# Four-layer graph network on 64 graphs: the multiplication order of layers 1 and 2, the places of right operands and kept blocks, and bias and mask on GpSimd

## The chip, the cores and the metric

The kernel runs on one core of one Trainium2 chip. The time is device microseconds of one execution. The kernel before took 2791.32 us (median of 3 runs, 2790.5 to 2792.68).

TensorE (PE in the profile, PEld its weight loads) multiplies matrices, VectorE (DVE), ScalarE (ACT) and GpSimd (POOL) do the rest, and SyncE (SP) issues all the transfers. Each engine runs its own instructions in order and waits for the others by semaphores.

## The reference

The input `x` is 64 graphs of 256 nodes with 512 features, `adj` a 256x256 matrix for each graph. Each of four layers adds its result to `x`. All is in float32.

```python
# h = relu(layernorm(x)) ahead of each layer; x = x + layer(h, adj)
# layer 0
Wh = h @ W;  e = leaky_relu(Wh @ a1 + (Wh @ a2).T)
attention = softmax(where(adj > 0.5, e, NEG_INF), axis=1)
out = elu(attention @ Wh)
# layer 1
Ah = adj + eye;  dh = rsqrt(sum(Ah, -1))
out = relu((dh[:, None] * Ah * dh[None, :]) @ h @ kernel + bias)
# layer 2
mask = any(h != 0, -1)
out = relu(adj @ h @ kernel) * mask
# layer 3
out = relu(concat([h, (adj @ h) / max(deg, EPS)], -1) @ W.T)
```

## The kernel before

**Block products.** Every matrix product is made by the scheme of Strassen and Winograd on 2x2 blocks: 7 block products in place of 8, with sums on both sides. A left operand has seven places (`A11, A12, S1, A22, S2, S4, S3`, line 33), a right one too (`B11, T4N, B22, T1, T3, T2, B21`, line 36). The function `project` (line 533) issues the seven products into three PSUM banks `z`, `y` and `v`; `snap` copies a bank out while the sum in it goes on, `add` adds a bank to a block that was copied before, and `last` takes the final block straight from the bank. Where no places are given, the blocks copied out are kept in a tile `c` of their own (line 539).

**Two orders of multiplying.** A layer needs adjacency times `h` times weights.

- *Aggregated* (`aggregate`, line 472): first 8 matmuls of 128x128x256 give the transpose of adjacency times `h` in two banks (line 482); `left_sums` (line 458) copies it into a tile `xw` and makes its sums; then 7 products of two chunks, 14 matmuls, with the weights.
- *Turned* (`turn`, line 619, and `neighbours`, line 651): `h` is transposed in 32x32 blocks on VectorE, written to DRAM (`hd`, one transfer) and read back in turned order (`hw`, four transfers); 14 matmuls with the weights give the right operand `y`; `differences` (line 256) makes its sums; then a `Gathered` operand multiplies by the adjacency in 7 matmuls. The sums of the adjacency's blocks come from `block_sums` (line 671) on GpSimd, in tiles `aw`.

Before, layers 0, 2 and 3 are turned and layer 1 is aggregated, in every graph. Layer 3 has also the product of `h` with the other half of its weights in the same banks, 35 matmuls in all. In the first FIRST = 2 graphs (line 25) `h` of layer 0 is transposed by TensorE (line 722) and not through DRAM.

**Around the products.** `norm` (line 394) is the layernorm with relu. In layer 1, VectorE copies the blocks out with row scale and bias in one instruction (line 804), adds the others with `dh` (line 811), and adds relu of them to `xs` (line 816). In layer 0, `off` (line 750) is the mask of the softmax; `deg` and `mask` (lines 708 and 839) are small instructions of VectorE.

**The order of the instructions** comes from a planner (class `Plan`, line 47). Each instruction is recorded with an engine, an estimated duration and what it reads and writes. Durations are multiplied by STRETCH per engine (line 28). Due times come from the graph's number times APART, with the last LAST graphs pulled ahead by LATE (line 365). The planner then places all the instructions by list scheduling, with a fixed number of buffers for each kind of tile (line 890), and they are issued in the order of their planned starts. Engines, PSUM banks and buffers of many graphs so interleave: at any time several graphs are in work.

Of the kernel before, what the change touches and what calls it, by code (L numbers as in the profile page):

```python
# [24 lines left out]
FIRST = 2  # L25
LAST, LATE = 2, 0.5

STRETCH = {"DVE": 1.1, "ACT": 1.03, "POOL": 1.25, "PE": 1.0, "DMA": 1.0}
# [7 lines left out]
B11, T4N, B22, T1, T3, T2, B21 = range(7)  # L36
# [117 lines left out]
def kernel(  # L154
# [39 lines left out]
    class Tiles:  # L194
# [61 lines left out]
    def differences(op, engs, tile, key, late=()):  # L256

        steps = ((slice(T1, T3 + 1), slice(B12, B22 + 1), slice(B11, B12 + 1), (B11, B12, B22), (T1, T3)),
                 (T2, B22, T1, (B22, T1), (T2,)),
                 (T4N, B21, T2, (B21, T2), (T4N,)))  # L260
        for (eng, us), (to, i, j, reads, writes) in zip(engs, steps):
            on = nc.vector if eng == "DVE" else nc.gpsimd
            op(eng, us, lambda g, on=on, to=to, i=i, j=j: on.tensor_tensor(  # L263
                tile(g)[:, to], tile(g)[:, i], tile(g)[:, j], ALU.subtract),
               [key(n) for n in reads], [key(n) for n in writes], **dict(late))
# [97 lines left out]
    def graph(b):  # L363
# [83 lines left out]
        def more_sums(xw):  # L447
            put = lambda *n: [f"{xw}.{i}" for i in n]
            op("DVE", 0.43, lambda g: nc.vector.tensor_tensor(  # L449
                g[xw][:, S2], g[xw][:, S1], g[xw][:, A11], ALU.subtract),  # L450
               put(S1, A11), put(S2), urgent=True)
            flat = lambda t: t.rearrange("p b k n -> p b (k n)")
            op("POOL", 1.45, lambda g: nc.gpsimd.tensor_tensor(  # L453
                flat(g[xw][:, S4 : S3 + 1]), flat(g[xw][:, A12 : A22 + 1 : A22 - A12]),
                flat(g[xw][:, S2 : S2 + 1]).to_broadcast([P, 2, FH * P]), ALU.subtract),
               put(A12, A22, S2), put(S3, S4), urgent=True)

        def left_sums(lo, hi, xw):

            declare(xw, [P, 7, FH, P], tag="xw")  # L460
            put = lambda *n: [f"{xw}.{i}" for i in n]
            op("ACT", 0.59, lambda g: nc.scalar.copy(
                g[xw][:, A12 : A22 + 1 : A22 - A12].rearrange("p h k n -> p k h n"),
                g[hi].rearrange("p k (h n) -> p k h n", h=NC)), [hi], put(A12, A22), urgent=True)
            op("ACT", 0.38, lambda g: nc.scalar.copy(g[xw][:, A11], g[lo][:, :, :P]),
               [lo], put(A11), urgent=True)
            op("DVE", 0.43, lambda g: nc.vector.tensor_tensor(
                g[xw][:, S1], g[lo][:, :, P:], g[xw][:, A22], ALU.add),
               [lo] + put(A22), put(S1), urgent=True)
            more_sums(xw)  # L470
# [23 lines left out]
        PLACE = {(0, 0): 0, (0, 1): 1, (1, 1): 2}  # L494

        class Weighted:


            def __init__(self, x, w):
                self.x, self.w, self.chunks = x, w, FH  # L500

            def left(self, g, at, k):
                return g[self.x][:, at, k]
# [7 lines left out]
        class Gathered:  # L511
# [21 lines left out]
        def project(operands, l, keep, keep_us, total, last, also=[], places=None, width=OH):  # L533
# [3 lines left out]
            if places is None:  # L537
                kept = f"c{l}"
                declare(kept, [P, 3, OH], tag="c")
                places = {ij: (lambda g, at=at: g[kept][:, at], f"{kept}.{ij[0]}{ij[1]}")  # L540
                          for ij, at in PLACE.items()}
# [52 lines left out]
        def both(t):  # L594

            return t[:, 0:2].rearrange("p a o -> p (a o)")

        def pieces(l):  # L600
            kept = f"c{l}"
            if l < 3:
                declare(f"total{l + 1}", [P, 3], tag="total")
            return (
                (1, "10", lambda g: g[f"pz{l}"], [f"pz{l}"], lambda g: quarter(g["xs"], 1, 0), ["xs.10"], 256, 1),
                (1, "11", lambda g: g[kept][:, 2], [f"{kept}.11"], lambda g: quarter(g["xs"], 1, 1), ["xs.11"], 256, 2),
                (0, "0", lambda g: both(g[kept]), [f"{kept}.00", f"{kept}.01"], lambda g: g["xs"][:, 0, :], ["xs.00", "xs.01"], 512, 0),
            )
# [10 lines left out]
        def turn(l):  # L619


            h, hw = f"h{l}", f"hw{l}"
            for c in (1, 0):
                op("DVE", 0.71, lambda g, c=c: nc.vector.transpose(g[h][:, c, :], g[h][:, c, :]),  # L624
                   [f"{h}.{c}"], [f"{h}.{c}"])
            hd, G = f"hd{l}", P // Q
            declare(hd, [N * F], tag="hd")
            op("DMA", 512, lambda g: nc.sync.dma_start(
                g[hd].rearrange("(p x) -> p x", p=P), g[h].rearrange("p c f -> p (c f)")),
               [f"{h}.0", f"{h}.1"], [hd], holds=0.45, lands=5.0)  # L630
            declare(hw, [P, 7, FH, P], tag="xw")
            for q in range(G):
                op("DMA", 128, lambda g, q=q: nc.sync.dma_start(
                    g[hw][q * Q : (q + 1) * Q, : 2 * NC].rearrange("j s k (a r) -> j (s k) a r", r=Q),
                    g[hd].rearrange("(a j x q r) -> q j x a r", a=G, j=Q, q=G, r=Q)[q]),
                   [hd], [f"{hw}.q{q}"], holds=0.85, lands=4.5)
            op("DVE", 0.48, lambda g: nc.vector.tensor_tensor(
                g[hw][:, S1], g[hw][:, S1], g[hw][:, A22], ALU.add),
               [f"{hw}.q{q}" for q in range(G)], [f"{hw}.{i}" for i in (A11, A12, A22, S1)], urgent=True)
            more_sums(hw)  # L640
# [10 lines left out]
        def neighbours(l, w, by=None, x=None, width=OH):  # L651


            y = f"y{l}"
            declare(y, [P, 7, width], tag="y")
# [10 lines left out]
            project([Weighted(x or f"hw{l}", w)], f"y{l}", keep, 0.38, total, last, also, places=places,  # L666
# [4 lines left out]
        def block_sums(l, a):  # L671
# [5 lines left out]
                g[aw][:, 0], block(g, 0, 1), block(g, 1, 1), ALU.add), [a] + ([f"h{l}.0"] if l else []), [f"{aw}.{S1}"])  # L677
# [30 lines left out]
        op("DVE", 0.18, lambda g: nc.vector.tensor_scalar_max(g["deg"], g["deg"], EPS_DEG),  # L708
# [41 lines left out]
        op("DVE", 0.48, lambda g: nc.vector.tensor_scalar(  # L750
# [19 lines left out]
        def elu0(i, key, y, y_keys, to, to_keys, n, at, tag):  # L770
            us = 0.42 if n == 256 else 0.61
            ex = f"ex{tag}"
            declare(ex, [P, n], tag=f"ex{n}")
# [10 lines left out]
        first, second, third = pieces(0)  # L784
        block_sums(0, "e")
        project([Gathered("e", "aw0", "y0")], 0, plain_keep, 0.38, plain_total, lambda _: elu0(*first, "a"))
# [8 lines left out]
            flat(g["ahT"])[:, P : 3 * P], flat(g["aT"])[:, P : 3 * P]), ["aT", "total1.0"], ["ahT.off"])  # L795
        for c in range(NC):
# [3 lines left out]
               ["aT", "=ident", "total1.0"], [f"ahT.{c}"])  # L800
        aggregate("h1", "ahT", 1, ["ahT.off", "ahT.0", "ahT.1"])
# [6 lines left out]
        def scaled_keep(i, j):  # L808
            return "DVE", lambda g, to, block: scaled(g, i, to, block, j)

        scaled_total = (0.49, lambda g, i, to, block: nc.vector.scalar_tensor_tensor(
            to, block, g["dh"][:, i : i + 1], to, ALU.mult, ALU.add))
# [7 lines left out]
        first, second, third = pieces(1)  # L820
# [6 lines left out]
        project([Weighted("xw1", 1)], 1, scaled_keep, 0.49, scaled_total, last1, ["dh", "=bias"])  # L827
# [11 lines left out]
        op("DVE", 0.17, lambda g: nc.vector.tensor_scalar(g["mask"], g["mask"], 0.0, None, ALU.is_gt),  # L839
# [3 lines left out]
        turn(2)  # L843
        neighbours(2, 2)
        block_sums(2, "aT")
# [9 lines left out]
        _, second, third = pieces(2)  # L855
        keep, total = row_scaled("mask")
        project([Gathered("aT", "aw2", "y2")], 2, keep, 0.38, total, last2, ["mask.0", "mask.1"])
# [7 lines left out]
        block_sums(3, "aT")  # L865
# [9 lines left out]
        project([Weighted("hw3", 3), Gathered("aT", "aw3", "y3")], 3, keep, 0.38, total, last3, ["rdeg"])  # L875
        _, second, third = pieces(3)
# [11 lines left out]
    for b in range(B):  # L888
        graph(b)
    buffers = dict(  # L890
        xs=8, a_nat=1, ab=1, aT=6, h=3, mva=5, xw=3, c=3, off=1, junk=1, ex256=3, ex512=1,
        a_rows=1, a_cols=1, turned=1, row=16, hd=8, y=3, pl=1, ps=8,
# [37 lines left out]
```

## Time and profile before

| | before |
|---|---|
| median of 3 runs | 2791.32 us |
| the profiled execution | 2790.29 us |
| its span | 2788.5 us |
| granted TensorE clock, mean | 0.998 |
| DMA queue q1 | 1018668 packets, 313.56 MB, 48.1% of 16 engines' time |
| HBM | 180.23 MB read, 133.23 MB written |

Times in the profile are microseconds from the start of the span, unless marked ns. A group of instructions is given by line, engine, operation, tiles written and read (buffer numbers left out), shape and count; then its busy time, the mean of one in ns, and the idle time of its engine just before. A float32 matmul leaves two records in the trace, so counts of MATMUL are twice the matmuls that the kernel issues.

### The profile page before, as it was taken

The numbers are of one execution on the slowest core, as the hardware profiler recorded it, in microseconds if no ns is written. First come the engines' busy times: TensorE is split into PE (matmuls) and PEld (weight loads), VectorE is DVE, ScalarE is ACT, GpSimd is POOL, SyncE is SP. The second block draws the span as 40 slices with busy tenths as digits, with TensorE's granted clock in tenths as the row PEclk, the third lists the DMA queues.
The fourth block names the chain that finished last, engine by engine and source line by source line (L and its number), as shares of the span: only waits on it lengthen the run. The fifth ranks groups of instructions, "written<-read, shape, count | busy, mean of one in ns | idle before, by whom it ended". The sixth has DMA issues, their size and how long they took to land.

```text
span 2788.5 us, 43020 instructions
## 1 busy us (share of the span) xinstructions
PE 2766.1 (99%) x12775; PEld 2423.6 (87%) x12775; DVE 2217.1 (80%) x5305; ACT 1782.1 (64%) x4318; POOL 1464.1 (53%) x2582
## 2 busy tenths in 40 slices
PE   7999999999999999999999999999999999999999
PEld 6888888888888888888888888888888888888887
DVE  6887788778887878878788787887878878778765
ACT  5776666665666666666666666665666666666653
POOL 6764545455454555555455454554645546455542
PEclk9999999999999999999999999999999999999999
DMA  8344454445454444544455444554544545444333
GB/s 223 81 119 118 102 114 118 114 113 124 99 129 115 105 114 107 136 115 106 105 120 119 114 108 112 122 114 108 128 100 120 126 102 131 99 114 98 78 91 76
DMA packets 1018901, 316.31 MB, mean 113 GB/s; under 512 B 933668, under 2 KB 960940, under 8 KB 1018668
## 3 DMA queue, kind: packets, MB, share of 16 engines
q1 hardware_dynamic: 1018668, 313.56, 48.1%
q8 instruction: 103, 1.69, 0.3%
q14 instruction: 130, 1.06, 0.1%
HBM read 180.23 MB, written 133.23 MB: 112 GB/s over the span
## 4 chain that ended last, share of the span: by engine, by line
PE 98%; DVE 1%; DMA 0%; SPq 0%; ACT 0%; issue 0%; POOL 0%; DVEq 0%; POOLq 0%; ACTq 0%
PE pz L551 28%; PE pzy L551 24%; PE pv L551 14%; PE pvy L551 12%; PE pt L482 8%; PE py L551 7%; PE pyy L551 6%; PE pwa_w L318 0%; DMA a_rows_w<-in_L_gnn_a_dram 0%; DMA w3n_w<-in_L_gnn_W_dram 0%; DVE e L752 0%; DVE y L263 0%; DVE h L624 0%; SPq L691 0%; DVE y L592 0%
## 5 line engine op out<-in xcount | busy, mean ns | idle before, releaser
L551 PE MATMUL pzy<-wb,hw 128*128 128x257 f32 (+1 forms) x3040 | 772.0, 380 | 2.7 <-DMA hw<-hd 2.2
L551 PEld LDWEIGHTS pzy<-wb,hw 128*128 128x128 f32 x3040 | 577.3, 190 | 83.1 <-issue 2.6
L443 ACT ACTIVATE h<-xs,nb,rstd 128x512 f32<-128x512 f32 x512 | 398.9, 807 | 34.3 <-POOL nb L440 28.7
L551 PE MATMUL pvy<-wb,hw 128*128 128x256 f32 (+1 forms) x1520 | 382.6, 380 | 0.0
L590 ACT COPY y<-pzy 128x256 f32<-128x256 f32 (+1 forms) x512 | 190.7, 372 | 281.7 <-PE pzy L551 232.7
L551 PEld LDWEIGHTS pvy<-wb,hw 128*128 128x128 f32 x1520 | 289.2, 190 | 40.5 <-DVE y L647 0.4
L453 POOL TENSOR_TENSOR hw<-hw 128x512 f32<-128x512 f32 x190 | 255.4, 1344 | 129.7 <-DVE hw L449 76.2
L422 ACT ACTIVATE h<-xs,mv 128x512 f32<-128x512 f32 x384 | 274.8, 716 | 21.6 <-POOL mv L416 14.1
L624 DVE STREAM_TRANSPOSE h<-h 128x512 f32<-128x512 f32 x380 | 257.3, 693 | 36.0 <-ACT h L443 36.0
L551 PE MATMUL pz<-wb,xw 128*128 128x256 f32 x1024 | 263.0, 379 | 0.8 <-DVE c L804 0.5
L551 PE MATMUL pz<-wb,hw 128*128 128x256 f32 x1024 | 262.8, 379 | 0.6 <-ACT c L645 0.6
L263 POOL TENSOR_TENSOR y<-y 128x256 f32<-128x256 f32 x192 | 156.9, 824 | 171.8 <-DVE y L263 116.3
L482 PE MATMUL pt<-ahT,h 128*128 128x256 f32 x1024 | 237.8, 381 | 2.0 <-POOL y L263 2.0
L263 DVE TENSOR_TENSOR y<-y 128x256 f32<-128x256 f32 (+1 forms) x384 | 231.3, 628 | 7.0
L551 PE MATMUL pz<-y,aw 128*128 128x256 f32 x768 | 228.4, 379 | 0.0
L551 PE MATMUL pv<-y,aw 128*128 128x256 f32 x768 | 228.4, 379 | 0.0
L816 DVE SCALAR_TENSOR_TENSOR xs<-c,xs 128x256 f32<-128x256 f32 (+1 forms) x384 | 221.3, 578 | 3.8
L482 PEld LDWEIGHTS pt<-ahT,h 128*128 128x128 f32 x1024 | 195.6, 191 | 29.2 <-POOL y L263 2.2
L551 PEld LDWEIGHTS pz<-wb,xw 128*128 128x128 f32 x1024 | 194.0, 190 | 28.5 <-POOL rstd L426 0.9
L551 PEld LDWEIGHTS pz<-wb,hw 128*128 128x128 f32 x1024 | 194.2, 190 | 27.7 <-ACT c L645 1.0
L645 ACT ACTIVATE y<-pzy,rdeg 128x256 f32<-128x256 f32 x256 | 120.8, 472 | 143.5 <-PE pzy L551 127.1
L430 POOL TENSOR_TENSOR rstd<-rstd,minus_half 128x2 f32<-128x2 f32 x256 | 199.3, 779 | 19.5
(135 smaller groups left out, 5629.8 us busy)
## 6 DMA issues: line engine op xcount, KB each, us to landing
hd<-h SPq DMA_DIRECT2D x190, 512.0 KB, 2.8
hw<-hd SPq DMA_DIRECT2D x760, 128.0 KB, 3.3
xs<-in_x_dram SPq DMA_DIRECT2D x64, 512.0 KB, 5.3
out_dram<-xs SPq DMA_DIRECT2D x64, 512.0 KB, 3.9
ab<-in_adj_dram SPq DMA_DIRECT2D x256, 64.0 KB, 2.5
a_nat<-in_adj_dram SPq DMA_DIRECT2D x64, 256.0 KB, 3.4
pl<-dpl SPq DMA_DIRECT2D x61, 128.0 KB, 3.2
wb<-in_L_gnn_kernel_dram SPq DMA_DIRECT2D x8, 256.0 KB
```

What stands on the lines that cost most here:

```text
L263: op(eng, us, lambda g, on=on, to=to, i=i, j=j: on.tensor_tensor(tile(g)[:, to], tile(g)[:, i], tile(g)[:, j], ALU.subtract), [key(n) for ...
L422: op("ACT", 1.0, lambda g, c=c: nc.scalar.activation(g[h][:, c, :], g["xs"][:, c, :], AF.Square, bias=g[mv][:, 0, c : c + 1], accum_out=g[ ...
L430: op("POOL", 0.72, lambda g: nc.gpsimd.tensor_tensor(g[rs], g[rs], minus_half, ALU.pow), [rs, "=half"], [rs])
L443: op("ACT", 0.81, lambda g, c=c: nc.scalar.activation(g[h][:, c, :], g["xs"][:, c, :], AF.Relu, bias=g[nb][:, c : c + 1], scale=g[rs][:, c ...
L453: op("POOL", 1.45, lambda g: nc.gpsimd.tensor_tensor(flat(g[xw][:, S4 : S3 + 1]), flat(g[xw][:, A12 : A22 + 1 : A22 - A12]), flat(g[xw][:, ...
L482: nc.tensor.matmul(g[pt][:, kk, :], lhsT=g[h][:, c, k * P : (k + 1) * P], rhs=g[moving][:, c, :], start=(c == 0), stop=(c == NC - 1),)
L551: nc.tensor.matmul(g[t], lhsT=o.left(g, left, k), rhs=o.right(g, right, k), start=start and n == 0, stop=n == len(parts) - 1, skip_group_c ...
L590: return "ACT", lambda g, to, block: nc.scalar.copy(to, block)
L624: op("DVE", 0.71, lambda g, c=c: nc.vector.transpose(g[h][:, c, :], g[h][:, c, :]), [f"{h}.{c}"], [f"{h}.{c}"])
L645: lambda i, j: ("ACT", lambda g, to, block: nc.scalar.activation(to, block, AF.Copy, scale=g[by][:, i : i + 1])),
L816: lambda g, kw: nc.vector.scalar_tensor_tensor(to(g), y(g), 0.0, to(g), ALU.max, ALU.add, **kw), y_keys, to_keys,
```

## The change

Five things change.

1. Layer 1 is turned in graphs 8 to 61 and aggregated in the others; layer 2, turned in all before, is now turned in graphs 8 to 61 and aggregated in the first eight and the last two.
2. Right operands of layers 1 and 2 are written into the places of the left operand `hw` that was used up (`y = f"hw{l}"`), and the kept blocks into places of an operand already used (`kept`); the tile `c` is gone. The places of the right operand are ordered anew, with T1 and T3, B11 and T4N, T4N and B22 two places apart. Block sums of the adjacency are made once for layers 2 and 3 in the turned graphs (`aw2`).
3. From graph 8 on, ScalarE copies layer 1's blocks with the row scale, and GpSimd adds the bias (`biased`).
4. On GpSimd in place of VectorE: `off` from graph 8 on, the maximum of `deg`, the comparison of `mask`.
5. The planner's figures: FIRST 3, LAST 3, LATE 0.3, STRETCH, and the buffers (`aT` 7, `xw` 4, no `c`, `ex256` 2).

```diff
-FIRST = 2
-LAST, LATE = 2, 0.5
-STRETCH = {"DVE": 1.1, "ACT": 1.03, "POOL": 1.25, "PE": 1.0, "DMA": 1.0}
+FIRST = 3
+LAST, LATE = 3, 0.3
+STRETCH = {"DVE": 1.06, "ACT": 1.06, "POOL": 1.15, "PE": 1.0, "DMA": 1.0}
...
-B11, T4N, B22, T1, T3, T2, B21 = range(7)
+B11, T1, T4N, T3, B22, T2, B21 = range(7)
...
-        steps = ((slice(T1, T3 + 1), slice(B12, B22 + 1), slice(B11, B12 + 1), (B11, B12, B22), (T1, T3)),
+        steps = ((slice(T1, T3 + 1, 2), slice(B12, B22 + 1, 2), slice(B11, B12 + 1, 2), (B11, B12, B22), (T1, T3)),
...
         class Weighted:
+                self.kept = x, (A11, S1, S2)
...
         class Gathered:
+                self.kept = y, (B11, T1, T3)
...
             if places is None:
-                kept = f"c{l}"
-                declare(kept, [P, 3, OH], tag="c")
-                places = {ij: (lambda g, at=at: g[kept][:, at], f"{kept}.{ij[0]}{ij[1]}")
-                          for ij, at in PLACE.items()}
+                kept, at = operands[-1].kept
+                places = {ij: (lambda g, n=n: g[kept][:, n, :OH], f"{kept}.{n}")
+                          for ij, n in zip(((0, 0), (0, 1), (1, 1)), at)}
...
                 op(eng, keep_us, lambda g: fn(g, at(g), g[f"p{bank}{l}"]),
                    [f"p{bank}{l}"] + also, [key], urgent=True)
+                if kept_then:
+                    kept_then(i, j, at, key)
...
-            y = f"y{l}"
-            declare(y, [P, 7, width], tag="y")
+            if l in (1, 2):
+                y = f"hw{l}"
+            else:
+                y = f"y{l}"
+                declare(y, [P, 7, width], tag="y")
...
-        op("DVE", 0.18, lambda g: nc.vector.tensor_scalar_max(g["deg"], g["deg"], EPS_DEG),
+        op("POOL", 0.3, lambda g: nc.gpsimd.tensor_scalar_max(g["deg"], g["deg"], EPS_DEG),
...
-        op("DVE", 0.48, lambda g: nc.vector.tensor_scalar(
+        op(*(("POOL", 1.0) if b >= 8 else ("DVE", 0.52)), lambda g: (nc.gpsimd if b >= 8 else nc.vector).tensor_scalar(
             g["off"], g["aT"], 0.5, 0.5, ALU.is_gt, ALU.subtract), ["aT"], ["off"])
...
-        aggregate("h1", "ahT", 1, ["ahT.off", "ahT.0", "ahT.1"])
+        if 8 <= b < B - 2:
+            turn(1)
+            neighbours(1, 1)
+            block_sums(1, "ahT")
+            operands = Gathered("ahT", "aw1", "hw1")
+        else:
+            aggregate("h1", "ahT", 1)
+            operands = Weighted("xw1", 1)
...
+        def biased(i, j, at, key):
+            op("POOL", 0.8, lambda g: nc.gpsimd.tensor_tensor(
+                at(g), at(g), bias[:, j * OH : (j + 1) * OH], ALU.add), [key, "=bias"], [key], urgent=True)
...
-        project([Weighted("xw1", 1)], 1, scaled_keep, 0.49, scaled_total, last1, ["dh", "=bias"])
+        if b >= 8:
+            keep, total = row_scaled("dh")
+            project([operands], 1, keep, 0.48, total, last1, ["dh"], kept_then=biased)
+        else:
+            keep = lambda i, j: ("DVE", lambda g, to, block: scaled(g, i, to, block, j))
+            total = row_scaled("dh")[1]
+            project([operands], 1, keep, 0.49, total, last1, ["dh", "=bias"])
...
-        op("DVE", 0.17, lambda g: nc.vector.tensor_scalar(g["mask"], g["mask"], 0.0, None, ALU.is_gt),
+        op("POOL", 0.3, lambda g: nc.gpsimd.tensor_scalar(g["mask"], g["mask"], 0.0, None, ALU.is_gt),
...
-        turn(2)
-        neighbours(2, 2)
-        block_sums(2, "aT")
+        if 8 <= b < B - 2:
+            turn(2)
+            neighbours(2, 2)
+            block_sums(2, "aT")
+            gathered = Gathered("aT", "aw2", "hw2")
+        else:
+            aggregate("h2", "aT", 2)
+            gathered = Weighted("xw2", 2)
...
-        block_sums(3, "aT")
+        if not 8 <= b < B - 2:
+            block_sums(2, "aT", 3)
...
-        xs=8, a_nat=1, ab=1, aT=6, h=3, mva=5, xw=3, c=3, off=1, junk=1, ex256=3, ex512=1,
-        a_rows=1, a_cols=1, turned=1, row=16, hd=8, y=3, pl=1, ps=8,
+        xs=8, a_nat=1, ab=1, aT=7, h=3, mva=5, xw=4, off=1, junk=1, ex256=2, ex512=1, a_rows=1,
+        a_cols=1, turned=1, row=16, hd=8, y=3, pl=1, ps=8,
```

More of the change, by code (lines that the diff above doesn't have):

```diff
@@ L451, in more_sums @@
                put(S1, A11), put(S2), urgent=True)
-            flat = lambda t: t.rearrange("p b k n -> p b (k n)")
             op("POOL", 1.45, lambda g: nc.gpsimd.tensor_tensor(
-                flat(g[xw][:, S4 : S3 + 1]), flat(g[xw][:, A12 : A22 + 1 : A22 - A12]),
-                flat(g[xw][:, S2 : S2 + 1]).to_broadcast([P, 2, FH * P]), ALU.subtract),
+                g[xw][:, S4 : S3 + 1], g[xw][:, A12 : A22 + 1 : A22 - A12],
+                g[xw][:, S2 : S2 + 1].to_broadcast([P, 2, FH * P]), ALU.subtract),
                put(A12, A22, S2), put(S3, S4), urgent=True)
         def left_sums(lo, hi, xw):
-            declare(xw, [P, 7, FH, P], tag="xw")
+            chunks = lambda t: t.rearrange("p (k n) -> p k n", k=FH)
+            declare(xw, [P, 7, OH], tag="xw")
             put = lambda *n: [f"{xw}.{i}" for i in n]
             op("ACT", 0.59, lambda g: nc.scalar.copy(
-                g[xw][:, A12 : A22 + 1 : A22 - A12].rearrange("p h k n -> p k h n"),
+                g[xw][:, A12 : A22 + 1 : A22 - A12].rearrange("p h (k n) -> p k h n", k=FH),
                 g[hi].rearrange("p k (h n) -> p k h n", h=NC)), [hi], put(A12, A22), urgent=True)
-            op("ACT", 0.38, lambda g: nc.scalar.copy(g[xw][:, A11], g[lo][:, :, :P]),
+            op("ACT", 0.38, lambda g: nc.scalar.copy(chunks(g[xw][:, A11]), g[lo][:, :, :P]),
                [lo], put(A11), urgent=True)
             op("DVE", 0.43, lambda g: nc.vector.tensor_tensor(
-                g[xw][:, S1], g[lo][:, :, P:], g[xw][:, A22], ALU.add),
+                chunks(g[xw][:, S1]), g[lo][:, :, P:], chunks(g[xw][:, A22]), ALU.add),
                [lo] + put(A22), put(S1), urgent=True)
@@ L492, in aggregate @@
             left_sums(f"pt{l}_0", f"pt{l}_1", f"xw{l}")
-        PLACE = {(0, 0): 0, (0, 1): 1, (1, 1): 2}
         class Weighted:
@@ L500, in __init__ @@
                 self.x, self.w, self.chunks = x, w, FH
+                self.kept = x, (A11, S1, S2)
             def left(self, g, at, k):
-                return g[self.x][:, at, k]
+                return g[self.x][:, at, k * P : (k + 1) * P]
             def right(self, g, at, k):
@@ L531, in keys, with project @@
                 return [of, f"{self.y}.{right}"]
-        def project(operands, l, keep, keep_us, total, last, also=[], places=None, width=OH):
+        def project(operands, l, keep, keep_us, total, last, also=[], places=None, width=OH,
+                    kept_then=None):
             if places is None:
-                kept = f"c{l}"
-                declare(kept, [P, 3, OH], tag="c")
-                places = {ij: (lambda g, at=at: g[kept][:, at], f"{kept}.{ij[0]}{ij[1]}")
-                          for ij, at in PLACE.items()}
+                kept, at = operands[-1].kept
+                places = {ij: (lambda g, n=n: g[kept][:, n, :OH], f"{kept}.{n}")
+                          for ij, n in zip(((0, 0), (0, 1), (1, 1)), at)}
             for t in "zyv":
@@ L592, in graph, with pieces @@
         plain_total = (0.43, lambda g, i, to, block: nc.vector.tensor_tensor(to, block, to, ALU.add))
[L594 to L601, printed above, removed]
+        def pieces(l, operands):
+            kept, (p00, p01, p11) = operands.kept
             if l < 3:
@@ L605, in pieces @@
                 (1, "10", lambda g: g[f"pz{l}"], [f"pz{l}"], lambda g: quarter(g["xs"], 1, 0), ["xs.10"], 256, 1),
-                (1, "11", lambda g: g[kept][:, 2], [f"{kept}.11"], lambda g: quarter(g["xs"], 1, 1), ["xs.11"], 256, 2),
-                (0, "0", lambda g: both(g[kept]), [f"{kept}.00", f"{kept}.01"], lambda g: g["xs"][:, 0, :], ["xs.00", "xs.01"], 512, 0),
+                (1, "11", lambda g: g[kept][:, p11, :OH], [f"{kept}.{p11}"], lambda g: quarter(g["xs"], 1, 1), ["xs.11"], 256, 2),
+                (0, "0", lambda g: g[kept][:, p00 : p01 + 1 : p01 - p00, :OH], [f"{kept}.{p00}", f"{kept}.{p01}"],
+                 lambda g: g["xs"][:, 0, :].rearrange("p (j o) -> p j o", o=OH), ["xs.00", "xs.01"], 512, 0),
             )
@@ L630, in turn @@
                [f"{h}.0", f"{h}.1"], [hd], holds=0.45, lands=5.0)
-            declare(hw, [P, 7, FH, P], tag="xw")
+            declare(hw, [P, 7, OH], tag="xw")
             for q in range(G):
                 op("DMA", 128, lambda g, q=q: nc.sync.dma_start(
-                    g[hw][q * Q : (q + 1) * Q, : 2 * NC].rearrange("j s k (a r) -> j (s k) a r", r=Q),
+                    g[hw][q * Q : (q + 1) * Q, : 2 * NC].rearrange("j s (a r) -> j s a r", r=Q),
                     g[hd].rearrange("(a j x q r) -> q j x a r", a=G, j=Q, q=G, r=Q)[q]),
@@ L664, in last @@
                    urgent=True)
-            project([Weighted(x or f"hw{l}", w)], f"y{l}", keep, 0.38, total, last, also, places=places,
+            project([Weighted(x or f"hw{l}", w)], f"h{l}", keep, 0.38, total, last, also, places=places,
                     width=width)
@@ L669, in neighbours, with block_sums @@
                         lambda i: f"{y}.{i}", dict(urgent=True))
-        def block_sums(l, a):
+        def block_sums(l, a, when=None):
             aw = f"aw{l}"
@@ L676, in block_sums @@
             op("POOL", 0.5, lambda g: nc.gpsimd.tensor_tensor(
-                g[aw][:, 0], block(g, 0, 1), block(g, 1, 1), ALU.add), [a] + ([f"h{l}.0"] if l else []), [f"{aw}.{S1}"])
+                g[aw][:, 0], block(g, 0, 1), block(g, 1, 1), ALU.add), [a] + ([f"h{when or l}.0"] if l else []), [f"{aw}.{S1}"])
             op("POOL", 0.5, lambda g: nc.gpsimd.tensor_tensor(
@@ L772, in elu0 @@
             ex = f"ex{tag}"
-            declare(ex, [P, n], tag=f"ex{n}")
+            declare(ex, [P, n] if n == OH else [P, n // OH, OH], tag=f"ex{n}")
             op("ACT", us, lambda g: nc.scalar.activation(g[ex], y(g), AF.Relu, scale=-1.0),
@@ L782, in elu0 @@
                 to(g), g[ex], -1.0, to(g), ALU.add, ALU.add, **kw), [ex], to_keys)
-        first, second, third = pieces(0)
+        gathered = Gathered("e", "aw0", "y0")
+        first, second, third = pieces(0, gathered)
         block_sums(0, "e")
-        project([Gathered("e", "aw0", "y0")], 0, plain_keep, 0.38, plain_total, lambda _: elu0(*first, "a"))
+        project([gathered], 0, plain_keep, 0.38, plain_total, lambda _: elu0(*first, "a"))
         elu0(*second, "b")
@@ L794, in graph @@
         op("POOL", 0.75, lambda g: nc.gpsimd.tensor_copy(
-            flat(g["ahT"])[:, P : 3 * P], flat(g["aT"])[:, P : 3 * P]), ["aT", "total1.0"], ["ahT.off"])
+            flat(g["ahT"])[:, P : 3 * P], flat(g["aT"])[:, P : 3 * P]), ["aT", "total1.0"], ["ahT.off", "ahT"])
         for c in range(NC):
@@ L799, in graph @@
                 flat(g["ahT"])[:, at], flat(g["aT"])[:, at], ident, ALU.add),
-               ["aT", "=ident", "total1.0"], [f"ahT.{c}"])
-        aggregate("h1", "ahT", 1, ["ahT.off", "ahT.0", "ahT.1"])
+               ["aT", "=ident", "total1.0"], [f"ahT.{c}", "ahT"])
+        if 8 <= b < B - 2:
[6 more added lines that the diff above has]
+            operands = Weighted("xw1", 1)
         def scaled(g, i, to, block, j):
@@ L806, in scaled @@
             )
[L808 to L812, printed above, removed]
+        def biased(i, j, at, key):
+            op("POOL", 0.8, lambda g: nc.gpsimd.tensor_tensor(
+                at(g), at(g), bias[:, j * OH : (j + 1) * OH], ALU.add), [key, "=bias"], [key], urgent=True)
         def relu_add(l, i, key, y, y_keys, to, to_keys, n, at):
@@ L818, in relu_add @@
                    urgent="pz3" in y_keys)
-        first, second, third = pieces(1)
+        first, second, third = pieces(1, operands)
         def last1(pz):
@@ L853, in last2 @@
                 ["v2"], ["xs.10"])
-        _, second, third = pieces(2)
+        _, second, third = pieces(2, gathered)
         keep, total = row_scaled("mask")
-        project([Gathered("aT", "aw2", "y2")], 2, keep, 0.38, total, last2, ["mask.0", "mask.1"])
+        project([gathered], 2, keep, 0.38, total, last2, ["mask.0", "mask.1"])
         relu_add(2, *second)
@@ L874, in graph @@
         keep, total = row_scaled("rdeg")
-        project([Weighted("hw3", 3), Gathered("aT", "aw3", "y3")], 3, keep, 0.38, total, last3, ["rdeg"])
-        _, second, third = pieces(3)
+        gathered = Gathered("aT", "aw2", "y3")
+        project([Weighted("hw3", 3), gathered], 3, keep, 0.38, total, last3, ["rdeg"])
+        _, second, third = pieces(3, gathered)
         relu_add(3, *second)
```

## The prediction

> **What bounds the kernel now.** I read the page's first part, its chain of waits, the busy time by stretch, TensorE's own waits, and last the groups by line with shapes kept apart.
>
> Busy time of each engine and the chain that ended last (page, parts 1 and 4):
>
> ```profile
> PE 2766.1 (99%) x12775; PEld 2423.6 (87%) x12775; DVE 2217.1 (80%) x5305; ACT 1782.1 (64%) x4318; POOL 1464.1 (53%) x2582
> ...
> PE 98%; DVE 1%; DMA 0%; SPq 0%; ACT 0%; issue 0%; POOL 0%; DVEq 0%; POOLq 0%; ACTq 0%
> ```
>
> TensorE (PE) is busy 99% of the span and is 98% of the chain. The 1% that it isn't lies at the ends. Busy time by stretch (from:to, length, then PE, PEld, DVE, ACT, POOL with instruction starts, granted clock, DMA share, GB/s):
>
> ```profile
> 24.00:46.00 22.00, 18.64 (x91) 14.13 (x89) 18.11 (x39) 14.75 (x42) 16.57 (x21) 1.00 0.88 236
> 46.00:52.00 6.00, 3.80 (x11) 2.94 (x10) 5.93 (x13) 2.88 (x9) 3.76 (x4) 0.72 1.00 219
> 52.00:59.00 7.00, 6.33 (x34) 4.78 (x33) 6.74 (x20) 6.47 (x21) 6.38 (x14) 1.00 1.02 241
> 59.00:67.00 8.00, 5.62 (x18) 4.47 (x19) 7.39 (x14) 6.02 (x17) 5.79 (x9) 0.79 0.71 172
> ...
> 80.00:150.00 70.00, 68.78 (x317) 59.27 (x316) 61.10 (x148) 53.76 (x134) 51.44 (x85) 1.00 0.37 78
> ...
> 400.00:2600.00 2200.00, 2200.00 (x10186) 1933.13 (x10185) 1777.58 (x4269) 1425.01 (x3444) 1151.02 (x2051) 1.00 0.49 114
> ```
>
> From 400 to 2600 us PE has no idle time at all. An f32 matmul leaves two records (the 512 of line 482 are a row of x1024), so one matmul costs 2 x 2200/10186 = 0.432 us there. A graph has 99 of them: 21 in layer 0, 22 in layer 1, 21 in layer 2, 35 in layer 3. That is 42.77 us a graph, 51.44 graphs in that stretch. So time is the number of matmuls times 0.432 us, plus what is lost at the ends.
>
> **The number of matmuls.** A turned layer multiplies by the weights first: 7 block products of 2 chunks, then 7 of 1 chunk, 21. An aggregated one spends 8 on line 482 and 14 on the weights, 22. Layer 1 goes from 22 to 21 in 54 graphs (8 to 61), layer 2 from 21 to 22 in the ten others: 44 fewer, 44 x 0.432 = **-19.0 us**. FIRST = 3 puts eight f32 transposes of graph 2 on PE; the row of line 722 has four of its records, two transposes, 0.44 us from start to start, so 8 x 0.22 = **+1.7 us**.
>
> **The middle.** This is taken as no new wait on PE, and the covers have to be shown. All per graph, with both layers turned, from the groups' means.
>
> VectorE has 1777.58/51.44 = 34.56 us. Off: three `c` of line 804 (3 x 0.477), the layer 1 sum of line 467 (0.412), `off` (0.524), `deg` (0.279), `mask` (0.187). On: two transposes (2 x 0.693), the sum of line 637 (0.507), three sums into `y` (3 x 0.420), two differences (0.732 + 0.524). Net +1.6, 36.1 us of a new period of 98 x 0.432 = 42.3: 85% against 81%.
>
> ScalarE has 27.70. Off: the two `xw` copies (0.590 + 0.372). On: four copies of the weights products (4 x 0.373), three scaled copies of line 645 (3 x 0.474). Net +2.0, 29.7 us, 70%.
>
> GpSimd has 22.38. On: a difference of line 263 (0.824), three bias adds, `off`, `deg`, `mask`. The bias add isn't in the trace; bounds are the 0.484 of a 128x128 add and the 1.344 of a 128x512 one, and I take 0.824, the same shape. For `off` on GpSimd the bounds are the 0.403 of the 128x256 copy and 1.344; I take 0.9, near twice the copy. The small ones are 0.3 each (line 416: 0.308). The sums of `aw1` come and those of `aw3` go. Net +4.8, 27.2 us, 64%; with all upper bounds 29.2, 69%.
>
> The queue: a turned layer issues one `hd` (0.32 us on the queue) and four `hw` (0.68 each), 3.0 us, four times a graph where it was three; DMA share 0.49 rises to at most 0.49 x 4/3 = 0.65. The further turn's transfers (2.8 and 3.3 us to landing) have to be covered by other graphs' products. In the order of the built program, between a layer's last product and the next turned layer's first weights product, PE had at least 62 matmuls (layer 2) and 57 (layer 3), and in the middle no wait. It now has at least 101, 81 and 65 (layers 1, 2, 3). If that cover were gone, a turn would show: two transposes, 2.8, 3.3 and the sums, some 9 us.
>
> Kept blocks in places of used operands add a wait of a write for a read; each such reader is a product issued earlier on PE than the one whose result is written, so the wait is over when the result is there. Step-2 slices in the differences: bounds 0 and 0.1 us on VectorE, which `y0` already shows with two separate runs; I take 0. The cost of the middle on PE: **0**, from 0 (TensorE can't be under its matmuls) to the first rival below.
>
> **The ends.** TensorE's own waits (total, times, longest):
>
> ```profile
> PE pzy L551 <- ACT y L590: 3.3, 5, 1.3
> PE pzy L551 <- DMA hw<-hd: 2.2, 1, 2.2
> PE pt L482 <- POOL y L263: 2.0, 1, 2.0
> ```
>
> The `hw` of this wait is graph 2's, which needs no transfer now. Between 24 and 150 us PE idles 3.4 + 2.2 + 0.7 + 2.4 + 1.2 = 9.8 us by the stretches, and after two of the waits it runs slowly:
>
> ```profile
> 48.35 1.94 PE L551 MATMUL pzy<-wb,hw 128*128 128x257 f32 x4 [2.20 <-DMA hw<-hd]
> 50.08 1.92 PE L551 MATMUL pvy<-wb,hw 128*128 128x257 f32 x4
> 51.79 1.09 PE L551 MATMUL pyy<-wb,hw 128*128 128x257 f32 x4
> ```
>
> Two matmuls take 1.73 us from start to start here, twice the usual, under a granted clock of 0.72; the two cold spells cost about 1.7 us each. [...]
>
> Bounds for the start: a gain of all 9.8 + 3.4 = 13 us, or a further wait like the `hw` one, a loss of 3.9. VectorE is 92 to 99% busy from 46 to 67 us, so a wait that is removed is mostly taken up by VectorE, and what counts is the work taken off it: graph 2 loses two transposes and line 637 and gains line 467 (-1.48), and about five graphs lose `deg` by then (5 x 0.279 = 1.4). I take **-3**. At the end PE has one wait of 0.6 us, and then the last sum, the last row and the output; the same stay: 0.
>
> **Sum.** The profiled execution took 2790.3 us (span 2788.5): -19.0 + 1.7 + 0 - 3 = -20.3, 2770.0. The median of the runs is 1.0 higher, so **2771 us**.
>
> **Rivals.**
> 1. *Copies late on ScalarE.* A product can only follow into a bank when the copy out of it is done. In the built order some 9 such copies a graph stand only three matmuls (1.30 us) ahead of the next product, where it was about 3. A copy takes 0.47 and a hop 0.05 on either side (PE to ACT to PE at 2780 us), so 0.72 us is left; one that finds a squaring (0.716 + 0.191) just begun is 0.19 late. Against it: such leads in the middle cost nothing before. For it: layer 1's copies are new on ScalarE, and ScalarE's own waits (line 443 for `nb`, up to 2.7 us) hold copies too. One a graph: 54 x 0.2 = 11, **2782 us**.
> 2. *The start gains most of its bound*: 12 instead of 3, **2762 us**. For it: graph 1's transposes now stand between graph 0's weights products, which had four of the waits for ACT. Against it: VectorE's load there.
> 3. *VectorE becomes the bound*, slower than before. These two rows differ only in where the second operand lies, SBUF or PSUM:
>
> ```profile
> L778 DVE SCALAR_TENSOR_TENSOR xs<-c,xs 128x256 f32<-128x256 f32 x64 | 35.7, 558 | 0.1
> L778 DVE SCALAR_TENSOR_TENSOR xs<-pz,xs 128x256 f32<-128x256 f32 x64 | 26.9, 420 | 12.7 <-ACT exa L774 7.0 <-PE pz L551 5.6
> ```
>
> With both in SBUF it is 138 ns dearer on average; single sums of line 637, of the same size, take 376 to 1023 ns in the middle. Summed over all such groups (mean less shortest usual) VectorE loses about 2.6 us a graph, 0.12 per us of GpSimd's 22.4; 4.8 more would make it 0.6 more, harmless. The upper bound is that each new GpSimd instruction holds VectorE for its whole length: 36.1 + 0.5 (idle without a cause) + 4.8 = 41.4 of 42.3. VectorE's waits are now 394 us in the middle, 7.7 a graph; if 1.3 of them couldn't be given up, the old period of 42.77 would be reached, and if 2.6, it is 44.0 and 54 x 1.25 = 68 us lost: **2859 us**. [...]
>
> **Chances.** Forecast 0.70, late copies 0.14, a better start 0.10, VectorE 0.06. The median can tell 0.2% (5.6 us) from no change. The late copies, spread about their price, are faster 0.09, same 0.04, slower 0.01: faster 0.89, same 0.04, slower 0.07. The range goes from the better start to just past the late copies, **2762 to 2783 us**, and leaves out VectorE and the worse half of the copies.
>
> **What would show it.** PE at 100% from 400 to 2600 us with 0.216 us a record, a period of 42.3 us; 6387 matmuls and transposes in place of 6423; no `hw` wait and one cold spell less before 80 us. VectorE near 85%, GpSimd near 64%. Wrong if PE waits for ACT `y`, `hw` or `c` copies in the middle (rival 1), or if PE idles there behind VectorE while VectorE has no waits (rival 3).

## The result, and the profile after

The changed kernel takes 2765.41 us (median of 4 runs, 2763.67 to 2765.6), the one before, on the same chip, 2790.91 us: ratio 0.9907, 95% interval 0.989 to 0.9924. That is 25.5 us less, where 20.3 were forecast, and inside the range of 2762 to 2783. The profiled execution took 2765.28 us, span 2763.5, so 25.0 us less than the profiled one before.

Busy time of each engine over the span (first part of the page of the changed kernel):

```profile
PE 2743.9 (99%) x12695; PEld 2407.4 (87%) x12695; DVE 2257.7 (82%) x5259; ACT 1870.5 (68%) x4576; POOL 1763.6 (64%) x2948
```

Busy time by stretch of the changed kernel (from:to, length, then PE, PEld, DVE, ACT, POOL with instruction starts, clock, DMA share, GB/s):

```profile
20.00:40.00 20.00, 19.44 (x92) 16.35 (x91) 12.84 (x26) 12.38 (x34) 16.66 (x19) 1.00 0.90 260
40.00:70.00 30.00, 24.30 (x110) 19.21 (x108) 27.68 (x74) 24.69 (x64) 23.12 (x41) 0.89 0.62 157
70.00:150.00 80.00, 80.00 (x376) 70.23 (x375) 64.98 (x152) 61.89 (x154) 55.81 (x94) 1.00 0.35 78
400.00:2600.00 2200.00, 2200.00 (x10186) 1933.08 (x10185) 1870.25 (x4345) 1520.21 (x3719) 1464.49 (x2434) 1.00 0.64 140
```

The same stretches at the start of the kernel before:

```profile
20.00:40.00 20.00, 16.76 (x69) 12.78 (x68) 13.32 (x31) 10.47 (x27) 14.77 (x18) 1.00 0.86 226
40.00:70.00 30.00, 24.62 (x109) 19.47 (x108) 28.10 (x62) 23.21 (x67) 24.23 (x33) 0.89 0.91 213
70.00:150.00 80.00, 78.78 (x364) 68.02 (x363) 69.79 (x169) 61.40 (x156) 58.31 (x95) 1.00 0.39 84
```

The middle reads as before: PE busy for the whole 2200 us, with the same 10186 records. It does as many matmuls in the same time, and a graph has one fewer, 98. The other engines carry more, and none of that reaches PE. In a period of 42.3 us VectorE has 36.0 us, ScalarE 29.3, GpSimd 28.2 (the busy times over 10186/196 = 51.97 graphs).

The rest is at the start. I add up, between starts of PE records that follow each other, what goes beyond 0.216 us for 256 columns (0.108 for the 128 columns of a transpose). This "loss" was 6.6 us from 20 to 40, 10.4 from 40 to 70 and 2.0 from 70 to 150 us; it is now 2.6, 9.5 and 0.0. So the start gives 7.3 us in all (0.4 of it before 20 us) and the end 0.8; one wait for `h` between 150 and 400 us takes 1.1 back. The counted work is 18.1 us: 19.0 for the matmuls, less 0.9 for the eight transposes. (A transpose leaves one record in the trace, and not two as a matmul does: the changed kernel has 12695 records and the one before 12775, so 88 fewer for 44 matmuls and 8 more for 8 transposes.) Together that is 25.1 us, where the profiled executions differ by 25.0.

### The profile page after: what moved, and what is told of

Its sections match the earlier page's. It is cut to its first block, busy times and chain, and to the rows that moved or that the text cites. A ratio compares the mean times of both kernels' runs of the same rounds, so it can differ in the third digit from the quotient of the medians.

```text
span 2763.5 us, 44602 instructions
## 1 busy us (share of the span) xinstructions
PE 2743.9 (99%) x12695; PEld 2407.4 (87%) x12695; DVE 2257.7 (82%) x5259; ACT 1870.5 (68%) x4576; POOL 1763.6 (64%) x2948
## 4 chain that ended last, share of the span: by engine, by line
PE 98%; POOL 1%; DVE 0%; ACT 0%; DMA 0%; issue 0%; SPq 0%; DVEq 0%
PE pzh L552 29%; PE pz L552 25%; PE pvh L552 15%; PE pv L552 13%; PE pyh L552 7%; PE py L552 6%; PE pt L482 3%; PE pwa_w L318 0%; DMA wb<-in_L_gnn_W_dram 0%; DVE y L263 0%; ACT h L443 0%; POOL wb L263 0%; PE pt L725 0%; POOL y L263 0%; DVE y L595 0%
## 5 line engine op out<-in xcount | busy, mean ns | idle before, releaser
L552 PE MATMUL pzh<-wb,hw 128*128 128x256 f32 (+1 forms) x3728 | 923.3, 379 | 0.0
L552 PEld LDWEIGHTS pzh<-wb,hw 128*128 128x128 f32 x3728 | 708.2, 190 | 98.4
L552 PE MATMUL pvh<-wb,hw 128*128 128x256 f32 (+1 forms) x1864 | 478.3, 379 | 0.0
L552 PEld LDWEIGHTS pvh<-wb,hw 128*128 128x128 f32 x1864 | 353.7, 190 | 49.1
L624 DVE STREAM_TRANSPOSE h<-h 128x512 f32<-128x512 f32 x466 | 314.3, 691 | 12.1 <-ACT h L443 12.1
L593 ACT COPY hw<-pzh 128x256 f32<-128x256 f32 x432 | 159.7, 370 | 182.5 <-PE pzh L552 181.5
L552 PE MATMUL pyh<-wb,hw 128*128 128x256 f32 (+1 forms) x932 | 239.5, 379 | 0.0
L263 DVE TENSOR_TENSOR y<-y 128x512 f32<-128x512 f32 (+1 forms) x256 | 206.4, 806 | 5.3
L552 PEld LDWEIGHTS pyh<-wb,hw 128*128 128x128 f32 x932 | 177.1, 190 | 24.3
L825 DVE SCALAR_TENSOR_TENSOR xs<-hw,xs 128x512 f32<-128x512 f32 (+1 forms) x216 | 159.6, 739 | 1.8
L263 DVE TENSOR_TENSOR hw<-hw 128x512 f32<-128x512 f32 x216 | 134.3, 622 | 26.5 <-PE pzh L552 22.6
```

Of the source, the lines that this page charges most:

```text
L552: nc.tensor.matmul(g[t], lhsT=o.left(g, left, k), rhs=o.right(g, right, k), start=start and n == 0, stop=n == len(parts) - 1, skip_group_c ...
L593: return "ACT", lambda g, to, block: nc.scalar.copy(to, block)
L825: lambda g, kw: nc.vector.scalar_tensor_tensor(to(g), y(g), 0.0, to(g), ALU.max, ALU.add, **kw), y_keys, to_keys,
```

## Experiments

Each kernel's time is set against runs of the kernel before on the same chip (2789.7 to 2790.4 us median). The kernels didn't all run on one chip, so a difference of 1 us between two of them means nothing. In the tables, "lost" in the middle is 2200 us less 0.216 us for each PE record from 400 to 2600 us.

### Is the gain the count of matmuls?

```diff
# changed kernel
-        if 8 <= b < B - 2:
+        if False:
             turn(1)
```

> The changed kernel with layer 1 aggregated in all 64 graphs, all else as changed. Theory (TensorE is the bound everywhere in the middle, and the gain is the count of its matmuls): 54 matmuls come back, 54 x 0.432 = 23.3 us on 2765.4, so 2789 us (2785 to 2792), no wait of TensorE from 400 to 2600 us. Rival (the gain comes from the planner's figures, the start and the relief of VectorE, not from the count): 2765 to 2775 us.

2788.15 us, ratio 0.9993 (0.9984 to 1.0002). That is 22.7 us above the changed kernel (24 by the two ratios), where 54 matmuls are 23.3. In the middle it has 10183 records, so nothing is lost there, and its start loses 12.5 us from 20 to 150 us, like the changed kernel's 12.1. Layer 1's order is worth its matmuls and no more.

### Where does the start gain?

Four kernels, each from the kernel before: the planner's figures; these and FIRST = 3; layer 2 aggregated in the ten graphs; all of these.

```diff
# old_with_new_figures
-LAST, LATE = 2, 0.5
-STRETCH = {"DVE": 1.1, "ACT": 1.03, "POOL": 1.25, "PE": 1.0, "DMA": 1.0}
+LAST, LATE = 3, 0.3
+STRETCH = {"DVE": 1.06, "ACT": 1.06, "POOL": 1.15, "PE": 1.0, "DMA": 1.0}
# old_with_first_3: besides
-FIRST = 2
+FIRST = 3
# old_l2_aggregated: this alone; old_l2_agg_new_figures: all of it
+        if 8 <= b < B - 2:
             turn(2)
...
+        else:
+            aggregate("h2", "aT", 2)
+            gathered = Weighted("xw2", 2)
```

> The kernel before with the planner's figures LAST, LATE and STRETCH of the changed one, FIRST = 2 kept. Theory (the 6 to 7 us that the start gained come from graphs 1 and 2 standing otherwise, and not from these figures): 2791 us, within 2 us. Rival (lower estimates give an order with fewer holes at start and end, and that is the surplus over the matmul count): 2783 to 2786 us.

> As the run before it, and FIRST = 3. Theory (graph 2 needs no transfer any more, so its wait of 2.2 us and the half rate after it go, and transposes fill the waits among graph 0's products; 8 transposes cost 1.7): 2 to 5 us faster than the run before it. Rival (VectorE's load from 46 to 67 us sets the start, and the waits only move): within 1 us of it, or slower by the 1.7 us of the transposes.

> The kernel before with layer 2 aggregated in the first eight and the last two graphs, all figures as before. Ten matmuls more, 4.3 us. Theory (layer 2's turning in the first graphs, its transposes on VectorE and transfers, is what holds up the start): the loss of the start over the matmuls' own time falls from 33.5 us to about 27, in all 2788 to 2790 us. Rival (the start depends on the order as a whole, not on this part): no fall, 2795 us or more.

> As old_l2_aggregated, with the planner's figures and FIRST = 3 of the changed kernel. Theory (these figures are no worse once layer 2 is aggregated at the start): start as in the changed kernel, 2788 to 2793 us. Rival (the figures need the changed kernel's buffers and VectorE's relief): slow at the start as old_with_first_3 was, 2805 us or more.

| kernel | us | ratio (95%) | loss 20-40 | 40-70 | 70-150 us |
|---|---|---|---|---|---|
| before | 2790 | | 6.6 | 10.4 | 2.0 |
| old_with_new_figures | 2804.22 | 1.0052 (1.0038-1.0066) | 6.1 | 7.5 | 13.4 |
| old_with_first_3 | 2813.97 | 1.009 (1.0076-1.0103) | 2.8 | 17.5 | 11.5 |
| old_l2_aggregated | 2796.38 | 1.0022 (1.0013-1.0031) | 4.9 | 10.9 | 1.8 |
| old_l2_agg_new_figures | 2796.76 | 1.0019 (1.0011-1.0028) | 2.9 | 14.4 | 1.2 |
| changed | 2765.41 | 0.9907 (0.989-0.9924) | 2.6 | 9.5 | 0.0 |

None of the four theories held. The figures alone cost 14 us, and FIRST = 3 on top 10 more; neither was expected to cost more than 2. For `old_l2_aggregated` the rival was right: the start hardly gets better, and the kernel is 6 us slower, 4.3 of it for ten more matmuls. `old_l2_agg_new_figures` lies between its theory and its rival. In parts the pairs still tell something. In this table the loss from 20 to 40 us is 2.6 to 2.9 with FIRST = 3, against 4.9 to 6.6 without: in the changed kernel graph 1's transposes stand between graph 0's products, and graph 2's between graph 1's, where the kernel before had waits for copies. It is the order that does this and not the figure alone, for `bias_back_other_order` below has FIRST = 3 and loses 7.3 there. Without the rest of the change this came back from 40 to 70 us, 17.5 after 7.5. Layer 2 aggregated takes away what the new figures lose from 70 to 150 us (13.4 and 11.5, then 1.2). What brings the stretch from 40 to 70 us down from 14.4 to 9.5 in the changed kernel (buffers, places, `deg` and `mask` on GpSimd) was not separated; the places were not tried alone at all.

### Does the count go on paying at the ends?

```diff
# changed kernel, three places
-        if 8 <= b < B - 2:
+        if 2 <= b:
```

> The changed kernel with layers 1 and 2 turned in graphs 2 to 63 in place of 8 to 61: 16 matmuls fewer, 6.9 us. Theory (the count alone decides): 2758.5 us. Rival (the start and the tail have no other graphs to cover the transfers and VectorE's transposes): what the count gives is lost again in new waits before 150 us or after 2650 us, 2765 us or more.

2823.75 us, ratio 1.0118 (1.0104 to 1.0132): 16 matmuls fewer and 58 us slower than the changed kernel. The loss is 27.9 us from 20 to 150, 11.0 from 150 to 400, 10.4 in the middle and 29.2 after 2600 us. The largest single piece, from the timeline of PE in this kernel:

```profile
2797.11 2.04 PE L552 MATMUL pzh<-wb,hw 128*128 128x256 f32 x4 [15.46 <-DMA hw<-hd]
```

This is layer 3 of the last graph, which is turned in every kernel here: layer 2's last product stands just before the wait, and no other graph is left to multiply. From the start of its `hd` (2788.12) to the end of the wait are 9.0 of the 15.46 us; before that come the last sums, the layernorm and the transposes. PE then starts at half rate (1.83 us from this row to the next, where four records usually take 0.87). Fewer matmuls pay here only where other graphs' products cover the waits. The rival is right on the time, though the longest wait isn't in a layer that the edit turns.

### Does the gain need the work that went to GpSimd?

All of it back on VectorE; the same with a lower estimate for VectorE; bias alone back; `off` alone back; all back, with the 32x32 transposes of layers 0 and 1 left out from graph 8 on.

```diff
# changed kernel
-        if b >= 8:
+        if False:
             keep, total = row_scaled("dh")
# off, deg, mask back, for example
-        op("POOL", 0.3, lambda g: nc.gpsimd.tensor_scalar_max(
+        op("DVE", 0.18, lambda g: nc.vector.tensor_scalar_max(
# back_on_dve_low_estimate, besides
-STRETCH = {"DVE": 1.06,
+STRETCH = {"DVE": 1.0,
# back_less_transposes, in turn, besides the first two
-            for c in (1, 0):
+            for c in () if l < 2 and b >= 8 else (1, 0):
```

> The changed kernel with bias, off, deg and mask back on VectorE in all graphs. Theory (TensorE bounds the middle; 2.4 us more on VectorE make it about 38.7 to 39 of a period of 42.3 us): 2765 us, 2762 to 2769, no wait of TensorE in the middle. Rival (VectorE is so near to its limit that the moves were needed for the gain): waits of TensorE behind VectorE in each of 54 graphs, at least 0.35 us each, 2784 us or more.

> Bias, off, deg and mask back on VectorE as in work_back_on_dve, and the planner's factor for VectorE 1.00 in place of 1.06. Theory A (the 100 us were lost by the order: at 1.06 the planner reckons some 43.6 us of VectorE a graph, more than the 42.3 of TensorE, and paces everything by VectorE, which really needs about 37): with 41.1 reckoned the order is paced by TensorE again, 2765 to 2775 us, idle time of TensorE from 400 to 2600 us under 5 us. Theory B (VectorE itself is the bound, through its waits and the instructions that GpSimd holds up): the waits of TensorE stay, 2840 us or more.

> The changed kernel with layer 1's copies and bias in one instruction on VectorE again, off, deg and mask left on GpSimd: VectorE 36.0 + 1.4 = 37.4 us a graph. Theory B (VectorE's load is what holds TensorE up, some 37 us a graph being all it can do in 42.3 us with its waits in order): waits in the middle, part of the 100 us, 2800 to 2860 us. Theory C (the place of layer 1's copies: a product that follows such a copy waits for VectorE's queue): nearly all of it, 2850 us or more. Neither: 2765 us.

> The changed kernel with off back on VectorE alone: VectorE 36.0 + 0.5 = 36.5 us a graph. Theory B: a small loss, 2766 to 2785 us, with a few waits of TensorE in the middle. Theory C: none, 2765 us within 2.

> As work_back_on_dve (bias, off, deg, mask on VectorE, factor 1.06), with the 32x32 transposes of layers 0 and 1 left out from graph 8 on (four of 0.69 us a graph; the output is another one): VectorE 37.2 to 37.3 - 2.8 = 34.5 us a graph, the moved work still on it. Theory B: back to 2765 to 2775 us, TensorE without idle time in the middle. Theory C: layer 1's copies still wait in VectorE's queue, 2830 us or more.

The first was 100 us slower than the changed kernel, and the lower estimate didn't help: theory A fell. Then `off` alone cost nothing. Bias alone cost 65 us, which is in B's range and less than C forecast. But with less work on VectorE it got worse still, 163 us, and B can't explain that. Theory C, the copies on VectorE, was left, though PE seldom waited for VectorE. PE's own waits in the middle of `only_bias_back` (total, times, longest):

```profile
PE pz L552 <- ACT y L645: 11.1, 20, 0.6
PE pzh L552 <- DMA hw<-hd: 6.4, 1, 6.4
PE pzh L552 <- ACT y L645: 4.2, 3, 1.7
PE pv L552 <- POOL aw L679: 3.4, 6, 0.7
PE pzh L552 <- ACT y L593: 2.1, 1, 2.1
```

Most of these are short waits for copies by ScalarE (21 of the 36 us of the whole list), largely in layers that the edit doesn't touch, while ScalarE is 64% busy. So I looked at the built orders. In the slow kernels, PE's next product into a bank often stands directly behind the product whose copy it needs, or with one matmul between, too near for a copy of 0.47 us. There PE can only wait, however fast the others are. Such places are counted below, from 400 to 2500 us of PE's own work; the kernel before has none. (How a bank that passes from one layer to another is counted moves the larger counts, from 33 to 39 for `only_bias_back` and from 60 to 97 for the last row, and leaves 0 and 1 as they are.) That gave theory D and a test of it: the same instructions as `only_bias_back`, planned with other figures.

```diff
# only_bias_back
-STRETCH = {"DVE": 1.06,
+STRETCH = {"DVE": 1.0,
-        ..., ex256=2, ...
+        ..., ex256=3, ...
```

> As only_bias_back (layer 1's copies and bias on VectorE, the same instructions on every engine), but planned with a factor of 1.00 for VectorE and a third ex256 buffer. In the order built for only_bias_back 38 products in the middle stand right behind the product whose copy they need, or with one matmul between; in this order it is 1, in the changed kernel none. Theory D (not VectorE's work but the holes that the planner left in TensorE's order cost the time): TensorE loses under 10 us from 400 to 2600 us, where only_bias_back lost 59; the start has many such places, so the whole is 2775 to 2800 us. Theory C (copies on VectorE hold TensorE up): the middle loses 40 us or more again, 2820 us or more.

| kernel | us | ratio (95%) | records, middle | lost, us | near products | VectorE, us a graph |
|---|---|---|---|---|---|---|
| changed | 2765.41 | 0.9907 (0.989-0.9924) | 10186 | 0 | 0 | 36.0 |
| only_off_back | 2765.58 | 0.9913 (0.9897-0.993) | 10186 | 0 | 0 | 36.6 |
| bias_back_other_order | 2788.26 | 0.9993 (0.9983-1.0002) | 10150 | 8 | 1 | 36.7 |
| only_bias_back | 2830.48 | 1.0147 (1.0132-1.0162) | 9907 | 60 | 38 | 36.7 |
| work_back_on_dve | 2865.34 | 1.0272 (1.0258-1.0286) | 9769 | 90 | 41 | 37.2 |
| back_on_dve_low_estimate | 2869.83 | 1.0286 (1.0272-1.03) | 9781 | 87 | 79 | 37.7 |
| back_less_transposes | 2928.17 | 1.0495 (1.0478-1.0512) | 9471 | 154 | 86 | 35.8 |

The middle of `only_bias_back`, and then of `bias_back_other_order` (columns as above):

```profile
400.00:2600.00 2200.00, 2162.76 (x9907) 1873.70 (x9906) 1853.91 (x4393) 1409.58 (x3475) 1326.88 (x2215) 1.00 0.62 136
```

```profile
400.00:2600.00 2200.00, 2196.76 (x10150) 1921.88 (x10150) 1901.61 (x4491) 1461.30 (x3557) 1399.07 (x2274) 1.00 0.63 139
```

The same work on each engine, 36.7 us of VectorE a graph in both, and PE loses 8 us where it lost 60. The whole is 2788 us, as theory D had it, and C's 2820 is out. Its order is poor at the start (24.3 us lost from 20 to 150), so it is no better kernel. VectorE's load decides nothing here: 36.7 us go with little loss, 35.8 with the largest. In the middle the time is set by the order that the planner finds. Two limits remain. The run has a third `ex256` buffer, and what that buffer is worth by itself was not separated from the order. And near products are not the whole loss: by starts of records, some 28 of the 60 us of `only_bias_back` lie before records that waited for a copy by ScalarE (41 of them), and the rest are the wait for `hw` (6.4 us), GpSimd's sums `aw` (3.4) and many small gaps; what a lower clock adds to them was not measured (the granted clock is 0.994 over the whole run, 0.998 in the changed kernel). In `back_less_transposes` the largest group of waits is for `hw` (24.4 us in 17 waits). So the count warns of a bad order and doesn't give its price: 79 near products go with 87 us, 41 with 90. That the place of the bias bears on it is shown only in that several plans with it on VectorE came out with holes; why the planner leaves them is open.

## The prediction, step by step

**The count**: right. 54 matmuls put back cost 22.7 us against 23.3. The other term of the count, +1.7 for the eight transposes, was twice too large: the four records of the row that it was read from are four transposes, not two. In the changed kernel eight of them take 0.87 us (the first row of the timeline below, to the start of the second), and graph 2's eight come to +0.9.

**The middle, no new wait**: right. PE 2200.00 of 2200 with 0.216 us a record. VectorE was forecast at 36.1 us a graph and measured 36.0 (in part by luck: prices that rose and prices that fell cancel, as the last section shows), ScalarE 29.7 and 29.3, GpSimd 27.2 and 28.2, DMA share at most 0.65 and 0.64. One bound failed: `off` on GpSimd was put between 0.403 and 1.344 us. The groups of the changed kernel by line with shapes kept apart (count, busy, mean ns, idle before):

```profile
L753 POOL TENSOR_SCALAR off<-aT 128x512 f32<-128x512 f32 x56 | 130.5, 2330 | 2.1 <-DVE aT L698 1.3 <-DVE e L755 0.6 <-DVE rdeg L713 0.2
L820 POOL TENSOR_TENSOR hw<-hw,bias 128x256 f32<-128x256 f32 x162 | 118.8, 734 | 202.6 <-ACT hw L645 202.5
...
L753 DVE TENSOR_SCALAR off<-aT 128x512 f32<-128x512 f32 x8 | 3.8, 474 | 0.1
```

It takes 2.33 us, almost five times VectorE's 0.47; a copy was the wrong neighbour for it. Why it is so dear (it compares and then subtracts) was not tested. It cost no time: `only_off_back`, with `off` on VectorE, is as fast. The bias add, 0.734, was within its bounds.

**The start, -3**: the sign was right and the size too small, and that is most of the 5 us between forecast and result. It measured about -7. The step that failed was to price the start by VectorE's relief, "a wait that is removed is mostly taken up by VectorE". The timeline of PE in the changed kernel shows what happened:

```profile
27.36 1.03 PE L725 MATMUL pt<-ident,h 128*128 128x128 f32 x8
28.23 1.03 PE L552 MATMUL pzh<-wb,xw 128*128 128x257 f32 x4
...
53.40 0.70 PE L552 MATMUL pz<-y,e 128*128 128x256 f32 x2 [1.64 <-ACT e L747]
57.02 1.22 PE L552 MATMUL pz<-y,aw 128*128 128x256 f32 x2 [2.92 <-POOL aw L681]
58.03 1.06 PE L552 MATMUL pv<-y,aw 128*128 128x256 f32 x2
```

From 40 to 70 us the outcome is as reasoned: the `hw` wait is gone, and waits for `e` and `aw` of 1.64 and 2.92 us stand in its place, so that stretch gains 0.9 of a possible 10.4. But it is ScalarE and GpSimd that end these waits, not VectorE. The sum `aw` stood in GpSimd's queue behind work for layer 1:

```profile
54.64 0.83 POOL L798 COPY ahT<-aT 128x256 f32<-128x256 f32 x1
55.46 0.26 POOL L416 TENSOR_SCALAR mv<-total 128x1 f32<-128x1 f32 x1
55.69 0.86 POOL L802 TENSOR_TENSOR ahT<-aT,ident 128x128 f32<-128x128 f32 x2
56.51 0.45 POOL L681 TENSOR_TENSOR aw<-aw,e 128x128 f32<-128x128 f32 x1
```

One cold spell (a stretch at half rate, granted clock 0.50) is left where there were two, as forecast, but it is as long as both together: the mean granted clock from 40 to 70 us is 0.89 before and after. From 20 to 40 us, where VectorE was 67% busy (13.32 of 20), transposes stand where the waits for ScalarE's copies were, and the loss falls by 4.0 us, as the second rival said. From 70 to 150 us the last 2.0 go too.

**The end, 0**: it gained 0.8; the wait of 0.6 us for a copy is gone.

**The rivals.** Late copies: none; about nine copies a graph with three matmuls of room cost nothing, and the runs above show what happens with less room than that. A better start: partly, some 7 of its 12 us. VectorE as the bound: no, and the runs with 36.6 and 36.7 us put more on it than the change does. No run shows the term that its 41.4 us is added up from, each new instruction of GpSimd holding VectorE for its whole length: GpSimd went from 22.4 to 28.2 us a graph, and VectorE came out at 36.0, where 36.1 was forecast without such holding. What the middle of the kernel before shows is less: line 778's sum of `c` and `xs` on 128x256 took 0.63 us on average beside an instruction of GpSimd (27 of 51) and 0.40 without (24), the one of `pz` and `xs` 0.42 either way. What the rival warned of, a slower kernel, lies elsewhere: a figure or a part changed can leave a planned order that is worse, by 14 us (`old_with_new_figures` against the kernel before) to 163 us (`back_less_transposes` against the changed one). The forecast could leave this out only because the order of the changed kernel was at hand and had no near products in the middle.

## What to carry to other kernels

Where one engine is busy without a gap, as TensorE is here (2200.00 of 2200 us), a change is worth the instructions it takes off that engine (22.7 us for 54 matmuls, 23.3 by the count), if the order still leaves room between each product and its copy; that room can be counted in the built order before anything runs. With a planner or list scheduler, a change of one part is also a new order, so an experiment that moves one instruction measures both; keep the instructions and change only the order to tell them apart. Busy shares of VectorE in the middle, 79% in the slowest of these kernels and 87% in a fast one, said nothing about which of these kernels was slow.

## What the hardware showed that was not expected

`off`, a comparison and a subtraction on 128x512, took 2.33 us on GpSimd where a sum of two 128x512 operands took 1.28 (line 452). VectorE's difference of line 263 on 128x512 in `y`, with both operands in SBUF, was forecast at 0.732 us and took 0.982 on average in the changed kernel. That isn't the doing of `off` alone: with `off` on VectorE again the same group is slower still. The rows are of the changed kernel, the last one of `only_off_back`:

```profile
L263 DVE TENSOR_TENSOR y<-y 128x512 f32<-128x512 f32 x128 | 125.7, 982 | 2.7
L263 DVE TENSOR_TENSOR hw<-hw 128x512 f32<-128x512 f32 x108 | 88.5, 820 | 22.8 <-PE pzh L552 22.6
```

```profile
L263 DVE TENSOR_TENSOR y<-y 128x512 f32<-128x512 f32 x128 | 151.6, 1185 | 4.3
```

Nor is it the places two apart. In the middle of the changed kernel the `hw` differences that ran beside no instruction of GpSimd took 0.65 us on average (53 of 103; the contiguous ones of the kernel before took 0.69 without GpSimd beside them), and those that ran beside GpSimd's sum of line 452 took 1.01 (47). So the price goes with what GpSimd runs at the same moment, and that is again a matter of the order. The neighbouring groups got cheaper (line 637 from 0.507 to 0.424 us), so VectorE's sum came out as forecast.

TensorE's granted clock fell to half inside the wait of 2.92 us and not after it: the wait runs from 54.1 to 57.02 us, and the share is 0.82 from 54 to 55 us and 0.50 from 55 on. Waits of 0.50 and 1.64 us stand just before it. In the kernel before, the fall came at the end of a single wait of 2.20 us (0.74 from 48 to 49 us). So here the length of one wait didn't tell when the half rate began.
